# A row LSTM on one Trainium2 core: image preparation dealt out anew at the start, one more odd output kept in PSUM, one wait placed earlier

## The chip, the cores and the metric

The kernel runs on one core of one Trainium2 chip. The metric is device time in microseconds (us); less is better. Before the change it is 1946.57 us, the median of 3 runs (1944.31 to 1946.65). All times below are in us unless marked ns.

## The reference

```
x : (8, 96, 128, 128) float32
v   = group_norm(x, 32 groups, no affine)
its = conv_1x3(v, W_is * mask) + b_is          # along the row, causal mask, 4*96 channels
for each of the 128 image rows:                # lax.scan, carry h, c : (8, 96, 128)
    gates = conv_1x3(h, W_ss) + b_ss + its[row]
    f, i, o = sigmoid(three quarters); g = tanh(the fourth)
    c = f * c + i * g
    h = o * tanh(c)
out = x + h of every row
```

The recurrence over the 128 rows is the long part: each row needs the hidden state of the row above.

## The kernel before

**Tiling and halves.** The eight images are split into two halves of four (s = 0 and 1). A half-step is one row of one half; half-step n is row n/2 of a half, with the first half one row ahead (`LEAD = 1`, `place`, lines 443 to 448). There are 256 half-steps, numbered from -2, and the two halves alternate, so that one half's products run on TensorE beside the other half's gates. Channels lie on the partitions: 96 partitions of hidden state `hx`, and 32 partitions that hold normalised input channels ("shared" channels) so that one product contracts both. Even and odd pixels are separate; the 1x3 convolution is computed from sums and differences of them with fewer products: `vs` (total, S), `vf` (difference, F), `vo` (shifted odd differences, D1) and `ve` (shifted even differences, D0, in `te`). The rest of the input channels arrive as "own" images `xs`: for each image of a block of four rows, a widening normalisation (`widen`, line 349), a sum (`add_pixels`, line 366) and a difference (`subtract_pixels`, line 370), all on GpSimd.

**Half-step.** Three PSUM banks A, B, C collect the gates. Products named 0, 1, 2, 3 take `vo`, `vs`, `vf`, `ve`; P, Q, E take the own images. Each is cut in two by row groups of 64 partitions ("lanes", marked < and >), so two products run side by side. ScalarE copies a bank's left half with the bias (`copy`, cp, line 620); VectorE then makes the even half (`even`, lo, line 624) and the odd half (`odd`, hi, line 628), and the 0 and 3 products are added to them after that. Then come the sigmoids and tanhs on ScalarE (lines 633, 654, 659), the cell on VectorE (`forget` 664, `gated` 673, `cell` 686), with the even pixels' input product on GpSimd from half-step 3 on (`gated`, line 671), tanh of the cell (694), and the outputs (703). From half-step 2 on ("banked") the odd output is left in PSUM: ScalarE copies it from there into `hx` (`keep_odd`, co, line 714), and copies the shared odd channels beside it (`shared_odd`, uo, line 719), so that S and F of the next row read one operand from PSUM.

**Order.** The instruction order of TensorE, ScalarE, VectorE and GpSimd is written by hand; each engine takes its instructions in that order. SyncE's DMA queue is ordered by the framework. A string `PERIOD` lists what one pass does; pass (period) n mixes the products of half-steps n and n+1 (marked +) with the gates of n-1 (marked '). It begins `siBb' 2C< taCb' U loA taCa' hiA cpB siC' PA+> gtb' QB+< 2C> 0A<`. Here `U` is the place where the shared images listed for half-step n-1 are normalised, W3 the place of the last piece of n-1's own image and of the loads listed behind it ("rest"), W1+ and W2+ the first two pieces of n's own image. S', F', D1' and D0' make the operands of half-step n+1. Passes 2 to 253 run this string; the last half-steps run another one, and half-steps -2 to 1 are written out by hand between the statistics of the last images (`events`) and in a few `do(...)` lines after them.

**Image work.** `work(n)` says which shared images, which own image and which loads belong to half-step n. For n under 8 it comes from the table `FIRST`, otherwise from a rule; `LATER` adds three more pieces, for the first own image of the second half's next block, in passes 10, 12 and 14. `shared(...)` gives an image to GpSimd (line 349, written to `hx`), `beside(...)` to ScalarE (line 347). `finish(0)` and `finish(1)` do the own images of half-steps 0 and 1 in one go.

**Waits.** An instruction carries one wait on another engine; what else it has to wait for is put in a separate instruction ahead of it on its queue. In each of the passes 3 to 253 the product `0A<` waits for VectorE (hiA) in such a separate instruction and for GpSimd (`vo`) itself, and `2C<` has no wait of its own. `follow(a, b)` adds a wait of a for b.

## Time and profile before

| | |
|---|---|
| median of 3 runs | 1946.57 us (1944.31 to 1946.65) |
| profiled execution | 1946.32 us |
| its span, first to last instruction | 1944.5 us |
| mean granted TensorE clock | 0.993 |
| TensorE busy (PE, matmul records) | 1868.6 us, 96%, 16400 records |
| VectorE (DVE) busy | 1558.2 us, 80% |
| ScalarE (ACT) busy | 1677.9 us, 86% |
| GpSimd (POOL) busy | 1567.9 us, 81% |
| DMA | 242.87 MB, 125 GB/s in the mean |

How to read it: PE is TensorE's matmuls, PEld its weight loads (a float32 product leaves two records of each), SP is SyncE, which issues DMAs. In a timeline a row gives start, duration, engine, line of the kernel (L628), operation, output<-inputs, their shapes, and how many like it are merged (x2); in square brackets stand the idle time of the engine just before it and what ended that. In the chain of waits a row gives start, duration and what ran. In the table by stretch a row gives the stretch, its length, then for PE, PEld, DVE, ACT and POOL the busy time with the number of instructions, then the granted clock (1.00 is full speed), the DMA share and GB/s. In the list of DMA issues the last figure is the median time from issue to landing. The statistics of the eight images take about the first 140 us; the half-steps of the main order follow.

### The profile page before, as it was taken

The page shows a single profiled execution, that of the slowest core. Times are in us where ns is not written, and L with a number is a line of the kernel's source. Part 1 is how long each engine was busy: PE and PEld are TensorE (multiplying, and loading weights), DVE is VectorE, ACT ScalarE, POOL GpSimd, SP SyncE. Part 2 cuts the span into 40 slices and gives each one's busy share as a digit, 9 for nine tenths or more (in the row PEclk, how much of TensorE's full clock was granted, in tenths as well). Part 3 has the DMA queues.
Part 4 walks back from the last instruction along what each step waited for, and adds up shares of the span by engine and source line. Part 5 has one row for each costly group of instructions (what it writes and reads, how often), then busy time and mean ns, then how long its engine had stood idle before and what let it go on. Part 6 is the DMA issues. An engine that isn't in the chain of part 4 may idle for free.

```text
span 1944.5 us, 46633 instructions
## 1 busy us (share of the span) xinstructions
PE 1868.6 (96%) x16400; PEld 1736.9 (89%) x16400; DVE 1558.2 (80%) x4018; ACT 1677.9 (86%) x3961; POOL 1567.9 (81%) x2169
## 2 busy tenths in 40 slices
PE   3778999999999999999999999999999999999998
PEld 0447999999999999999999999999999999999996
DVE  5877888888888888888888888888888888888886
ACT  6687888888888888888888888888888888888887
POOL 4347888888888888888888888888888888888862
PEclk9989999999999999999999999999999999999999
DMA  9994344334434443444344334434443444344301
GB/s 405 413 303 101 90 120 123 104 96 124 114 93 105 124 113 99 109 121 106 88 120 123 104 97 122 115 92 105 123 113 98 109 121 109 86 121 123 93 28 45
DMA packets 110294, 242.87 MB, mean 125 GB/s; under 512 B 6832, under 2 KB 16368, under 8 KB 104048
## 3 DMA queue, kind: packets, MB, share of 16 engines
q1 hardware_dynamic: 110064, 239.89, 44.2%
q8 instruction: 133, 2.18, 0.5%
q14 instruction: 97, 0.79, 0.1%
HBM read 181.34 MB, written 50.33 MB: 119 GB/s over the span
## 4 chain that ended last, share of the span: by engine, by line
PE 92%; DMA 3%; DVE 2%; ACT 2%; POOL 1%; issue 0%; SPq 0%; DVEq 0%; POOLq 0%; ACTq 0%
PE ps L548 92%; DMA x<-in_x_dram 2%; DVE bst L1215 1%; DMA te<-in_x_dram 1%; POOL xw L349 0%; ACT g L633 0%; POOL xs L366 0%; PE rows L224 0%; ACT ps L654 0%; POOL xs L370 0%; PE pv L303 0%; POOL hx L349 0%; ACT o L659 0%; ACT xr L235 0%; ACT hx L268 0%
## 5 line engine op out<-in xcount | busy, mean ns | idle before, releaser
L548 PE MATMUL ps<-te,wl 64*128 64x256 f32 (+1 forms) x3042 | 911.6, 380 | 0.2
L548 PE MATMUL ps<-vf,wm 64*128 64x256 f32 (+1 forms) x3046 | 782.1, 382 | 0.1
L548 PE MATMUL ps<-vo,wl 64*128 64x256 f32 (+1 forms) x3042 | 738.3, 385 | 6.0 <-DVE ps L628 5.9
L548 PE MATMUL ps<-xs,wx 64*128 64x256 f32 (+1 forms) x3080 | 699.8, 377 | 2.1 <-POOL xs L366 1.8
L548 PE MATMUL ps<-vs,wm 64*128 64x256 f32 (+1 forms) x3046 | 658.0, 378 | 9.8 <-POOL vs L739 7.1
L548 PEld LDWEIGHTS ps<-te,wl 64*128 64x128 f32 (+1 forms) x3042 | 520.3, 186 | 42.5 <-PE ps L548 1.4
L624 DVE TENSOR_TENSOR ps<-m,ps 128x256 f32<-128x256 f32 x768 | 323.5, 421 | 279.4 <-ACT m L620 279.3
L548 PEld LDWEIGHTS ps<-xs,wx 64*128 64x128 f32 x3080 | 492.2, 187 | 14.5 <-POOL xs L366 3.4
L548 PEld LDWEIGHTS ps<-vo,wl 64*128 64x128 f32 (+1 forms) x3042 | 487.3, 186 | 18.0 <-DVE ps L628 8.4
L548 PEld LDWEIGHTS ps<-vf,wm 64*128 64x128 f32 (+1 forms) x3046 | 442.8, 185 | 32.1 <-PE ps L548 0.9
L548 PEld LDWEIGHTS ps<-vs,wm 64*128 64x128 f32 (+1 forms) x3046 | 446.5, 188 | 16.1 <-POOL vs L739 9.9
L620 ACT ACTIVATE m<-ps,wl 128x256 f32<-128x256 f32 x766 | 360.0, 470 | 24.9 <-PE ps L548 11.9
L633 ACT ACTIVATE g<-ps 32x512 f32<-32x512 f32 x765 | 317.9, 447 | 45.0 <-PE ps L548 10.2
L628 DVE TENSOR_TENSOR ps<-m,ps 128x256 f32<-128x256 f32 x768 | 325.5, 424 | 17.6
L548 PE MATMUL ps<-xs,wt 64*128 64x256 f32 x1012 | 299.2, 376 | 1.4 <-DVE ps L628 1.4
L370 POOL TENSOR_TENSOR xs<-xw 128x512 f32<-128x512 f32 (+1 forms) x254 | 294.0, 1158 | 0.1
L671 POOL TENSOR_TENSOR g<-i,g 96x256 f32<-96x256 f32 x251 | 182.4, 727 | 138.2 <-ACT g L633 137.9
L654 ACT ACTIVATE ps<-ps 96x512 f32<-96x512 f32 (+1 forms) x512 | 243.3, 475 | 45.5 <-PE ps L548 45.1
L349 POOL TENSOR_SCALAR xw<-xr,rstd,nmr 128x512 f32<-128x512 f32 (+1 forms) x267 | 210.3, 789 | 36.5 <-DVE nmr L341 11.5
L694 ACT ACTIVATE ps<-c 96x256 f32<-96x256 f32 x512 | 193.2, 378 | 40.1 <-DVE c L686 3.7
L753 POOL TENSOR_TENSOR vo<-hx 128x256 f32<-128x256 f32 x257 | 157.3, 612 | 84.4 <-ACT hx L714 74.9
L349 POOL TENSOR_SCALAR hx<-x,rstd,nmr 32x512 f32<-32x512 f32 x245 | 199.1, 813 | 27.5 <-ACT hx L347 2.1
(132 smaller groups left out, 2661.3 us busy)
## 6 DMA issues: line engine op xcount, KB each, us to landing
xr<-in_x_dram SPq DMA_DIRECT2D x124, 512.0 KB, 6.3
x<-in_x_dram SPq DMA_DIRECT2D x62, 768.0 KB, 4.9
out_dram<-x SPq DMA_DIRECT2D x62, 768.0 KB, 4.6
x<-in_x_dram SPq DMA_DIRECT2D x16, 1024.0 KB, 10.8
x<-in_x_dram SPq DMA_DIRECT2D x62, 256.0 KB, 2.9
xs<-in_x_dram SPq DMA_DIRECT2D x15, 1024.0 KB, 12.2
te<-in_x_dram SPq DMA_DIRECT2D x8, 1024.0 KB, 11.1
hx<-in_x_dram SPq DMA_DIRECT2D x8, 1024.0 KB, 9.6
```

Of the source, the lines that this page charges most:

```text
L349: return engine.tensor_scalar(dst, src, scale, shift, ALU.mult, ALU.add)
L370: return engine.tensor_sub(differences, strided(xw[:, 0, :], 0, [(W + 1, n), (J + 1, 2), (1, J)]), strided(xw[:, 0, :], J, [(W + 1, n), (0 ...
L548: made = nc.tensor.matmul(self.ps[a][:, bass.ts(half, HB)][:, cols], weights[rows, bass.ts(a, P)], rhs[rows, cols], start=new, stop=False, ...
L620: nc.scalar.activation(self.m1[a], m1, AF.Identity, bias=column)
L624: nc.vector.tensor_add(self.ps[a][:, 0:HB], self.m1[a], self.ps[a][:, HB:])
L628: nc.vector.tensor_sub(hi, self.m1[a], hi)
L633: made = nc.scalar.activation(self.part(g, lo, hi, t), self.part(ps, lo, hi, t), AF.Tanh)
L654: made = nc.scalar.activation(to, gate, AF.Sigmoid)
L671: nc.gpsimd.tensor_mul(to, i, g)
L694: nc.scalar.activation(th, self.part(self.c, lo, hi, t), AF.Tanh)
L753: nc.gpsimd.tensor_sub(to, h[:, :, 0:J], h[:, :, 1 : J + 1])
L1215: nc.vector.bn_stats(bst[:, done, :], xc[:, bass.ts(j, SN)])
```

## The change

Three edits.

1. The table `FIRST` and what follows it: no image is given to ScalarE any more (`beside` is gone); the own and shared images of half-steps 0 to 7 are dealt out differently; the first own image of the second half's next block (image 3 of block 1) is cut into three pieces that follow in passes 4, 5 and 6, image 1 of the first half's block 2 into pieces in passes 9, 10, 11, and image 0 of the second half's block 2 in passes 12, 13, 14. Two loads (`spare`, `load_rows` of the second half) move to the list of half-step 6, those of the first half from half-step 1 to 3.
2. `banked` from half-step 1 instead of 2, with `co uo` written into the hand order of half-step 1 after `ou`, ahead of F and S.
3. The first 2C product of each half-step waits for `vo`, the odd differences of GpSimd that `0A<` of the same half-step needs later.

```diff
-            self.banked = self.n >= NH
+            self.banked = self.n >= 1
...
+            if kind == "2" and a == order["C"] and first is None and "vo" in self.kept:
+                follow(self.made, self.kept["vo"], "the odd differences are there")
...
-            nc.gpsimd.tensor_sub(to, h[:, :, 0:J], h[:, :, 1 : J + 1])
+            self.kept["vo"] = nc.gpsimd.tensor_sub(to, h[:, :, 0:J], h[:, :, 1 : J + 1])
...
-    def beside(s, k, *images):
-        return shared(s, k, *images, engine=nc.scalar)
-
     FIRST = [
-        ([], own(0, 1, 1), own(0, 1, 2)),
-        (shared(0, 1, 0), own(0, 1, 3), [(spare, 0, 1), (load_rows, 0, 2)]),
-        (beside(0, 1, 1) + shared(0, 1, 2) + beside(0, 1, 3), own(1, 1, 0), [(load_shared, 0, 2)]),
-        (shared(1, 1, 0), own(1, 1, 1), []),
-        (beside(1, 1, 1) + shared(1, 1, 2), own(1, 1, 2), []),
-        (shared(1, 1, 3), own(1, 1, 3), [(spare, 1, 1), (load_rows, 1, 2), (load_shared, 1, 2)]),
-        (shared(0, 2, *SHARED[0]), own(0, 2, 0), [(load_shared, 0, 3)]),
-        ([], own(0, 2, 1), []),
+        ([], own(0, 1, 1), []),
+        (shared(0, 1, 0, 1), (), []),
+        (shared(0, 1, 2), own(0, 1, 2), [(load_shared, 0, 2)]),
+        (shared(0, 1, 3), own(0, 1, 3), [(spare, 0, 1), (load_rows, 0, 2)]),
+        (shared(1, 1, 0), own(1, 1, 0), []),
+        (shared(1, 1, 1), own(1, 1, 1), [(load_shared, 1, 2)]),
+        (shared(1, 1, 2) + shared(0, 2, 0), own(1, 1, 2), [(load_shared, 0, 3)]),
+        (shared(1, 1, 3), own(0, 2, 0), []),
     ]
-    LATER = dict(zip((9, 11, 13), own(1, 2, 0, 1)))
+    LATER = dict(
+        [*zip((3, 4, 5), own(1, 1, 3, 1)), *zip((8, 9, 10), own(0, 2, 1, 1)),
+         *zip((11, 12, 13), own(1, 2, 0, 1))]
+    )
+    BLOCK = {6: [(spare, 1, 1), (load_rows, 1, 2)]}
...
-            return FIRST[n]
+            channels, image, rest = FIRST[n]
+            return channels, image, rest + ([LATER[n]] if n in LATER else []) + BLOCK.get(n, [])
...
-    do(1, "gt th 0+A 3+A 0+B 3+B 0+C 3+C ou F S D0 D1 re")
+    do(1, "gt th 0+A 3+A 0+B 3+B 0+C 3+C ou co uo F S D0 D1 re")
```

`own(s, k, j, buffer)` returns the three pieces of own image j of block k of half s, `shared(s, k, j, ...)` the normalisations of shared images, as listed in the kernel above.

## The prediction

> **What bounds the kernel now.** I read the page first, then the engines' busy times by stretch, then the chain of waits from 155 to 200 us, then the timelines of the single engines there and in a later stretch for comparison.

> ```profile
> span 1944.5 us, 46633 instructions
> 160.00:170.00 10.00, 6.79 (x46) 5.82 (x47) 5.96 (x16) 6.94 (x15) 6.44 (x9) 0.90 0.87 181
> 168.00:169.00 1.00, 1.00 (x7) 0.95 (x6) 0.97 (x4) 0.97 (x3) 0.10 (x1) 0.50 1.10 211
> 180.00:190.00 10.00, 9.16 (x80) 8.16 (x80) 7.33 (x20) 8.52 (x20) 7.51 (x10) 1.00 0.27 64
> 400.00:800.00 400.00, 400.00 (x3655) 380.82 (x3653) 325.59 (x857) 352.18 (x857) 344.73 (x457) 1.00 0.41 107
> ```

> In the steady stretch (400 to 800) TensorE is never idle. From 160 to 190, in periods 3 to 6 of the hand-written order, it is: 46 matmul records between 160 and 170 where the steady stretch has 91 in ten microseconds, and between 168 and 169 the granted clock is 0.50. So an edit to the steady order has little to win, and the edits to periods 2 to 16 are priced in that start.

> The clearest ruler is line 628 for bank B (hiB), which runs once a period and lets the next odd products go:

> ```profile
> 166.41 0.42 DVE L628 TENSOR_TENSOR ps<-m,ps 128x256 f32<-128x256 f32 x1
> 174.95 0.41 DVE L628 TENSOR_TENSOR ps<-m,ps 128x256 f32<-128x256 f32 x1
> 183.49 0.41 DVE L628 TENSOR_TENSOR ps<-m,ps 128x256 f32<-128x256 f32 x1
> 190.50 0.42 DVE L628 TENSOR_TENSOR ps<-m,ps 128x256 f32<-128x256 f32 x1
> 246.55 0.42 DVE L628 TENSOR_TENSOR ps<-m,ps 128x256 f32<-128x256 f32 x1
> 253.81 0.42 DVE L628 TENSOR_TENSOR ps<-m,ps 128x256 f32<-128x256 f32 x1
> 260.81 0.41 DVE L628 TENSOR_TENSOR ps<-m,ps 128x256 f32<-128x256 f32 x1
> ```

> These are periods 3, 4, 5, 6, 14, 15 and 16. From 6 to 14 eight periods take 56.05, so a good period is 7.01. Period 4 takes 8.54 (1.53 too long), period 5 again 8.54 (1.53 too long), period 15 takes 7.26 (0.25 too long). The chain of waits says why periods 3 and 5 are late:

> ```profile
> 162.96 0.82 POOL hx L349
> 163.80 0.84 ACT hx L347
> 164.66 0.39 ACT g L633
> ...
> 180.49 0.85 ACT hx L347
> ...
> 181.50 0.81 POOL hx L349
> ...
> 182.40 0.73 POOL g L671
> ```

> ScalarE's share of the shared-channel images (L347, the helper "beside") writes the same tile as GpSimd's (L349), and each waits for the other in turn. The tanh (L633) that the cell needs stands behind them on ScalarE's queue.

> **The change part by part.**

> *The "beside" images go to GpSimd.* In period 3 the queues of ScalarE, VectorE and TensorE read:

> ```profile
> 160.54 0.38 ACT L633 ACTIVATE g<-ps 64x256 f32<-64x256 f32 x1
> 161.09 0.41 DVE L673 TENSOR_TENSOR g<-ps,g 96x256 f32<-96x256 f32 x1
> 166.88 0.70 PE L548 MATMUL ps<-vo,wl 64*128 64x256 f32 x4 [3.21 <-DVE ps L628]
> ```

> Without the two images the second tanh starts when the first ends, at 160.54 + 0.38 = 160.92 instead of 164.66: 3.74 earlier. VectorE then does gtb (161.09, done about 161.5) and goes on without its pause; the same chain of five VectorE operations leads to hiB, about 0.1 less is won because gtb stands in front, and another 0.1 goes to the PSUM edit below. That puts hiB at 162.9 instead of 166.41: 3.5 won. It cannot be less than about 3.2 (the idle time that TensorE's row shows) unless another wait takes the place, nor more than 3.7. What is late next is nothing: bank B's copy, which hiB also needs, follows the tanh on ScalarE as before. In period 5 the same pair (ScalarE 180.49, GpSimd 181.50, and the product 182.40 behind it) costs the 1.53 of that period; it goes too, because ScalarE has no image any more and GpSimd waits for none.

> *The clock.* Period 4 has no wait of its own; its 1.53 is the stretch at clock 0.50 that follows TensorE's 3.21 idle. Period 5's shorter stall leaves the clock at 1.00 (the row 180 to 190). So without the 3.21 I take the 1.53 as won; its ends are 0 and 1.53. [...]

> *GpSimd's new load.* It gets ScalarE's three images (0.81 to 0.85 each, on either engine) and the first images of the second half, one piece more in periods 4 (widen), 5 (add) and 6 (subtract), then 9, 10, 11 and 12, 13, 14; period 7 has two shared images in front of its gate product. What a piece too many does is shown by period 14, which has one subtraction more already:

> ```profile
> 245.41 0.73 POOL L671 TENSOR_TENSOR g<-i,g 96x256 f32<-96x256 f32 x1 [0.48 <-ACT g L633]
> ...
> 246.80 2.28 POOL L370 TENSOR_TENSOR xs<-xw 128x512 f32<-128x512 f32 x2
> 249.06 0.82 POOL L349 TENSOR_SCALAR xw<-xr,rstd,nmr 128x512 f32<-128x512 f32 x1
> ...
> 250.97 0.75 POOL L366 TENSOR_TENSOR xs<-xw 128x256 f32<-128x256 f32 x1
> 251.82 0.81 POOL L349 TENSOR_SCALAR hx<-x,rstd,nmr 32x512 f32<-32x512 f32 x1
> 252.71 0.72 POOL L671 TENSOR_TENSOR g<-i,g 96x256 f32<-96x256 f32 x1
> 253.47 0.42 DVE L686 TENSOR_TENSOR c<-ps,g 96x256 f32<-96x256 f32 x1 [0.15 <-POOL g L671]
> ```

> From gate product to gate product GpSimd needs 7.30 here without a pause, so 7.30 - 1.14 = 6.16 without the second subtraction (2.28 / 2), and 0.85 is free in a good period. The product came 0.29 late (7.30 - 7.01), VectorE waited for it, and hiB lost 0.25. So lateness of the gate product costs nearly its own length.
> - Periods 4 and 5: one widen (0.82) or one add (0.75) on 6.16 is at most 6.98, under 7.01: nothing.
> - Period 6 into 7: a subtraction (1.14) and a second shared image (0.81, with its handover 0.85) give 6.16 + 1.99 = 8.15. The product is 1.14 late, about 1.1 lost. Bounds: 0.7 if the pauses ahead can be worked into, 2 if every added piece costs 0.2 more.
> - Period 11 into 12: again 7.30, 0.25 lost, new. Period 14 into 15 is as before.

> *The odd output of half-step 1 stays in PSUM.* VectorE's last operations before TensorE goes on with the products of half-step 3, and the later forms:

> ```profile
> 155.08 0.75 DVE L703 TENSOR_TENSOR hx<-o,ps 96x256 f32<-96x256 f32 x2 [0.78 <-ACT ps L694]
> 155.86 1.18 DVE L743 TENSOR_TENSOR vf<-hx 128x256 f32<-128x256 f32 x1
> 156.96 0.41 DVE L739 TENSOR_TENSOR vs<-hx 128x256 f32<-128x256 f32 x1
> 166.99 0.38 ACT L719 ACTIVATE ps<-hx 32x256 f32<-32x256 f32 x1
> 176.46 0.42 DVE L743 TENSOR_TENSOR vf<-ps,hx 128x256 f32<-128x256 f32 x1
> ```

> Added are two ScalarE copies of 0.38 between the output products (they end at 155.83) and the difference; the difference falls from 1.18 to 0.42 with one operand in PSUM. 155.83 + 2 x 0.38 + 0.33 (the step from one such VectorE operation to the next) + 0.42 + some 0.2 of handovers is 157.54 against the 157.37 at which the sum ends now: 0.1 to 0.2 lost, already in the 3.5. I take 0.42, the row with the same operands; were the PSUM form as slow as 1.18 here, 0.9 would be lost. [...] The copies push the ScalarE work of half-step 2 back by about 1.3; ScalarE stands idle 2.45 after it, so nobody waits:

> ```profile
> 159.79 0.47 ACT L620 ACTIVATE m<-ps,wl 128x256 f32<-128x256 f32 x1 [2.45 <-PE ps L548]
> ```

> *The wait on GpSimd's odd differences moves from the odd product 0A to the first 2C product,* in every period. The separate VectorE wait in front of 0A goes, since one wait then fits the matmul itself.

> ```profile
> 312.45 0.61 POOL L753 TENSOR_TENSOR vo<-hx 128x256 f32<-128x256 f32 x1 [0.26 <-ACT hx L714]
> 314.75 0.34 PEld L548 LDWEIGHTS ps<-vf,wm 64*128 64x128 f32 x4
> 315.63 0.18 PEld L548 LDWEIGHTS ps<-vo,wl 64*128 64x128 f32 x1
> 603.10 0.38 PE L548 MATMUL ps<-vo,wl 64*128 64x256 f32 x1
> 606.77 0.38 PE L548 MATMUL ps<-vf,wm 64*128 64x256 f32 x1
> ```

> The differences end at 313.06 and the loads of 2C are at 314.75: 1.7 to spare (2.6 before), and even a GpSimd 1.1 late keeps 0.6. Queued behind the waiting product are all of TensorE's further products. From 603.10 (the first record of a 0A) to 606.77 TensorE starts 34 records, 0.1079 each; over the whole steady stretch it is 400 / 3655 = 0.1094. So all of TensorE's waits together take 64 x 0.0015 = 0.1 of a period of 64 records: the ends are -0.1 and +0.1 a period. I take 0, because both waits at 0A are met before its load is due.

> *Transfers.* The first block's spare rows and next rows go out later, in periods 4 and 7 on SyncE's queue:

> ```profile
> xr<-in_x_dram SPq DMA_DIRECT2D x124, 512.0 KB, 6.3
> ```

> They land in about 6.3 and are first read two periods (14) or more afterwards. Hidden; if they took over 13, GpSimd would wait.

> **Sum.** 3.5 + 1.53 + 1.53 - 1.1 - 0.25 = 5.2 won, against the profiled execution's 1946.32 (span 1944.5 and 1.8 around it): 1941.1. That run is 0.25 under the median of 1946.57, so 1941.4 for a median. A measurement here can tell about 0.2% (3.9) from no change.

> **The rivals.**
> - *GpSimd becomes the bound of the start.* Nine periods carry an added piece; if each costs 0.2 more than its row, periods 4, 5, 9 to 14 overrun too, by 0.1 to 0.25 each, and period 7 by 2. The win falls to 2.5 to 3.8: 1942.8 to 1944. For it: the free 0.85 lies in two pauses that ScalarE's results set. Against: periods 10 and 12 carry a piece more already, and from 6 to 14 the eight periods are all of 7.01 in the mean. Chance 0.18.
> - *The clock falls anyway:* the stretch at 0.50 belongs not to the 3.21 but to all of TensorE's idle time since 140, which stays in part. 1.5 less, 1942.9. For it: no row quoted here shows a second stall of that length with the same consequence. Against: the row 168 to 169 stands right behind the stall's end at 166.88. Chance 0.07. [...]
> - *The stall of period 7 hides* (GpSimd works ahead), or the shorter wait list speeds the steady order a little: 1939 to 1940. Chance 0.08.
> - *Slower: the moved wait is paid every period.* 2C's load comes where the queue has just waited for the other lane, so what stands there is not hidden. A wait of w adds 251 w, over periods 3 to 253. It decides from (5.2 + 3.9)/251 = 0.036; at 0.1, as much as all waits of a period now cost, it is 25 - 5.2, 1966. Against: the differences are 1.7 early, and a wait that is met shows no gap at 0A. Chance 0.05.
> - *The change does not do it:* the period 3 stall stays because GpSimd's own images stand before the gate product there. But that product is VectorE's in period 3. Chance 0.02.

> **How the numbers follow.** Forecast (1939.8 to 1942.7) 0.60. Faster: 0.60 + 0.08 and a small part of the first two rivals, 0.70. Same: the rest of these and the unchanged case, 0.25. Slower 0.05. The range takes the forecast, the third case and most of the first two: 1939.0 to 1944.6.

> **What would show it.** In the profile after: hiB of period 3 near 163 and no idle row of over 1 us before an odd product until period 7; no granted clock under 1.00 after 145; no ScalarE images of 32x512 after 152; a VectorE wait of about 1 us on GpSimd's gate product near 191; the difference at 0.42 near 156.8. The steady period stays 7.01. It is wrong if the period changes, if the clock still falls near 168, or if the periods 4 to 6 show waits on GpSimd.

## The result, and the profile after

| | before | after |
|---|---|---|
| median, nine runs each on one chip | 1945.49 us (1944.31 to 1946.84) | 1940.21 us (1939.25 to 1941.34) |
| profiled execution (its span) | 1946.32 (1944.5) | 1941.34 (1939.5) |
| mean granted clock | 0.993 | 0.994 |
| instructions | 46633 | 46380 |

The ratio is 0.9973, 95% interval 0.9964 to 0.9982: the changed kernel is faster by 0.27%, 5.3 us. In the kernel after, lines 620 to 771 stand two further down, so the bank B ruler (hiB, line 628) is L630 and the gate product of GpSimd (line 671) is L673.

The table by stretch of the kernel after, columns as before:

```profile
160.00:170.00 10.00, 9.94 (x82) 8.75 (x82) 7.37 (x20) 7.88 (x20) 7.67 (x10) 1.00 0.32 78
168.00:169.00 1.00, 1.00 (x12) 0.96 (x10) 0.06 (x1) 0.99 (x4) 0.90 (x3) 1.00 1.12 246
...
180.00:190.00 10.00, 10.00 (x95) 9.48 (x93) 7.72 (x21) 8.82 (x21) 9.69 (x14) 1.00 0.26 79
190.00:200.00 10.00, 9.67 (x85) 8.64 (x84) 7.56 (x20) 8.01 (x21) 8.90 (x12) 1.00 0.93 204
400.00:800.00 400.00, 400.00 (x3658) 380.87 (x3657) 325.18 (x857) 352.27 (x857) 344.81 (x458) 1.00 0.42 108
```

The hole between 160 and 170 is mostly closed (82 matmul records in place of 46), the half-rate microsecond at 168 is at 1.00, and 180 to 190 has the 95 records of a good stretch. (A row of ten microseconds counts records that begin before it too, so a full one has 95 and not the 91 of the long stretch, which the prediction set beside the 46.) One hole is left, or rather new: 190 to 200 has 85 records, ten too few, so about 1.1 us lost (10 x 0.11). The idle column there shows only 0.33 us. While one lane waits the last products of the other still run: one lane's end at 193.22 and the other's, on `te`, at 193.60, and the next record begins at 193.94, 0.72 behind the last start, where the steady stretch has 0.11. So the count of records is the better measure of this short stall.

The ruler, VectorE's timeline of the kernel after:

```profile
145.42 1.09 DVE L630 TENSOR_TENSOR ps<-m,ps 128x256 f32<-128x256 f32 x3
...
164.42 0.42 DVE L630 TENSOR_TENSOR ps<-m,ps 128x256 f32<-128x256 f32 x1
...
171.42 0.42 DVE L630 TENSOR_TENSOR ps<-m,ps 128x256 f32<-128x256 f32 x1
...
178.42 0.41 DVE L630 TENSOR_TENSOR ps<-m,ps 128x256 f32<-128x256 f32 x1
...
185.42 0.41 DVE L630 TENSOR_TENSOR ps<-m,ps 128x256 f32<-128x256 f32 x1
...
193.47 0.41 DVE L630 TENSOR_TENSOR ps<-m,ps 128x256 f32<-128x256 f32 x1
...
221.48 0.42 DVE L630 TENSOR_TENSOR ps<-m,ps 128x256 f32<-128x256 f32 x1
...
228.74 0.41 DVE L630 TENSOR_TENSOR ps<-m,ps 128x256 f32<-128x256 f32 x1
...
242.74 0.42 DVE L630 TENSOR_TENSOR ps<-m,ps 128x256 f32<-128x256 f32 x1
...
250.00 0.42 DVE L630 TENSOR_TENSOR ps<-m,ps 128x256 f32<-128x256 f32 x1
```

The hiB of period 2 is the second of the three in the first row, at 145.75; then follow those of periods 3, 4, 5, 6, 7, 11, 12, 14 and 15. Periods 4, 5 and 6 take 7.00 each; 7 takes 8.05, 12 takes 7.26 (228.74 - 221.48), 15 takes 7.26. In the kernel before, the hiB of period 2 is the second of the three in this row of VectorE, at 144.16:

```profile
143.83 1.08 DVE L628 TENSOR_TENSOR ps<-m,ps 128x256 f32<-128x256 f32 x3
```

So the main order begins 1.6 later in the profiled execution of after, for a reason that is not the change (last section). Absolute times of the two traces may not be set against each other; lengths from hiB to hiB may. That is the measure of everything below. From hiB of period 2 to that of period 17 before takes 123.66 and after 118.25: 5.41 won.

### The profile page after: what moved, and what is told of

The parts are those of the page before. It is cut to its first block, busy times and chain, and to the rows that moved or that the text cites. A ratio compares the mean times of both kernels' runs of the same rounds, so it can differ in the third digit from the quotient of the medians.

```text
span 1939.5 us, 46380 instructions
## 1 busy us (share of the span) xinstructions
PE 1866.1 (96%) x16400; PEld 1736.1 (90%) x16400; DVE 1554.4 (80%) x4018; ACT 1676.1 (86%) x3960; POOL 1567.1 (81%) x2172
## 4 chain that ended last, share of the span: by engine, by line
PE 92%; DMA 3%; ACT 2%; DVE 1%; POOL 1%; issue 0%; SPq 0%; DVEq 0%; POOLq 0%; ACTq 0%
PE ps L548 92%; DMA x<-in_x_dram 2%; DVE bst L1219 1%; DMA te<-in_x_dram 1%; POOL xw L349 0%; ACT g L635 0%; POOL xs L370 0%; ACT ps L656 0%; ACT x L269 0%; ACT x L268 0%; POOL xs L366 0%; PE pv L303 0%; ACT m L622 0%; ACT ps L696 0%; ACT o L661 0%
## 5 line engine op out<-in xcount | busy, mean ns | idle before, releaser
L548 PE MATMUL ps<-te,wl 64*128 64x256 f32 (+1 forms) x3042 | 909.6, 379 | 0.2
L548 PE MATMUL ps<-vf,wm 64*128 64x256 f32 (+1 forms) x3046 | 783.6, 382 | 0.1
L548 PE MATMUL ps<-vo,wl 64*128 64x256 f32 (+1 forms) x3042 | 736.4, 384 | 2.3 <-DVE ps L630 2.2
L548 PE MATMUL ps<-xs,wx 64*128 64x256 f32 (+1 forms) x3080 | 700.0, 377 | 3.4 <-POOL xs L366 1.8
L548 PE MATMUL ps<-vs,wm 64*128 64x256 f32 (+1 forms) x3046 | 657.8, 378 | 10.7 <-POOL vs L741 7.9
L548 PEld LDWEIGHTS ps<-te,wl 64*128 64x128 f32 (+1 forms) x3042 | 519.7, 185 | 42.6 <-PE ps L548 1.4
L548 PEld LDWEIGHTS ps<-vo,wl 64*128 64x128 f32 (+1 forms) x3042 | 495.7, 186 | 13.7 <-DVE ps L630 4.4
L548 PEld LDWEIGHTS ps<-xs,wx 64*128 64x128 f32 x3080 | 492.2, 187 | 16.2 <-POOL xs L366 3.4
L548 PEld LDWEIGHTS ps<-vf,wm 64*128 64x128 f32 (+1 forms) x3046 | 443.5, 186 | 32.2 <-PE ps L548 0.9
L548 PEld LDWEIGHTS ps<-vs,wm 64*128 64x128 f32 (+1 forms) x3046 | 445.9, 188 | 17.0 <-POOL vs L741 10.4
L630 DVE TENSOR_TENSOR ps<-m,ps 128x256 f32<-128x256 f32 x768 | 325.5, 424 | 17.6
L548 PE MATMUL ps<-xs,wt 64*128 64x256 f32 x1012 | 299.2, 376 | 1.4 <-DVE ps L630 1.4
L370 POOL TENSOR_TENSOR xs<-xw 128x512 f32<-128x512 f32 (+1 forms) x254 | 293.0, 1154 | 0.1
L673 POOL TENSOR_TENSOR g<-i,g 96x256 f32<-96x256 f32 x251 | 182.0, 725 | 133.7 <-ACT g L635 133.1
L349 POOL TENSOR_SCALAR xw<-xr,rstd,nmr 128x512 f32<-128x512 f32 (+1 forms) x267 | 209.3, 785 | 35.7 <-DVE nmr L341 11.5
L349 POOL TENSOR_SCALAR hx<-x,rstd,nmr 32x512 f32<-32x512 f32 x248 | 201.3, 812 | 25.8
## 6 DMA issues: line engine op xcount, KB each, us to landing
xr<-in_x_dram SPq DMA_DIRECT2D x124, 512.0 KB, 6.4
```

The costliest lines, as they stand in the source:

```text
L349: return engine.tensor_scalar(dst, src, scale, shift, ALU.mult, ALU.add)
L370: return engine.tensor_sub(differences, strided(xw[:, 0, :], 0, [(W + 1, n), (J + 1, 2), (1, J)]), strided(xw[:, 0, :], J, [(W + 1, n), (0 ...
L548: made = nc.tensor.matmul(self.ps[a][:, bass.ts(half, HB)][:, cols], weights[rows, bass.ts(a, P)], rhs[rows, cols], start=new, stop=False, ...
L630: nc.vector.tensor_sub(hi, self.m1[a], hi)
L673: nc.gpsimd.tensor_mul(to, i, g)
```

## The experiments

Theory A: the stall of period 3 and the clock that falls behind it, and the stall of period 5, all come from the two engines that write the shared images in turn (edit 1); GpSimd's extra pieces give 1.3 of it back; edits 2 and 3 are nearly nothing. Rivals: the gain is owed to the moved wait or to the odd output; the clock falls for another reason than the stall; the new order of the images, and not the engine that writes them, does it. After is set against the nine runs of before in the first table, wait only to after without wait against 25 other runs of it (median 1946.92), filled stall to engine only against 26 more (1945.63).

| kernel | median us (runs) | ratio to before, 95% | period 3 | 4 | 5 | 7 | 8 | 12 | 15 | 3 to 17 |
|---|---|---|---|---|---|---|---|---|---|---|
| before | | | 22.25 | 8.53 | 8.55 | 7.01 | 7.01 | 7.01 | 7.25 | 123.66 |
| after | 1940.21 (9) | 0.9973 (0.9964 to 0.9982) | 18.66 | 7.00 | 7.00 | 8.04 | 7.00 | 7.26 | 7.26 | 118.25 |
| wait only | 1946.11 (11) | 0.9998 (0.9989 to 1.0006) | 22.25 | 8.56 | 8.55 | 7.00 | 7.00 | 7.01 | 7.26 | 123.66 |
| table only | 1940.35 (5) | 0.9968 (0.9955 to 0.9980) | 18.59 | 7.00 | 7.00 | 8.05 | 7.00 | 7.26 | 7.27 | 118.21 |
| odd output only | 1945.75 (11) | 0.9995 (0.9986 to 1.0004) | 21.99 | 8.55 | 8.55 | 7.01 | 7.00 | 7.00 | 7.26 | 123.40 |
| after without wait | 1941.70 (9) | 0.9976 (0.9966 to 0.9985) | 18.66 | 7.00 | 7.00 | 8.06 | 7.00 | 7.27 | 7.26 | 118.28 |
| filled stall | 1944.38 (11) | 0.9994 (0.9985 to 1.0003) | 22.26 | 7.00 | 8.56 | 7.01 | 7.00 | 7.01 | 7.25 | 122.13 |
| one image later | 1941.12 (10) | 0.9975 (0.9966 to 0.9984) | 18.66 | 7.00 | 7.01 | 7.26 | 7.26 | 7.26 | 7.26 | 117.74 |
| spread | 1939.02 (5) | 0.9966 (0.9953 to 0.9978) | 18.66 | 7.01 | 7.00 | 7.00 | 7.01 | 7.00 | 7.01 | 116.74 |
| engine only | 1941.71 (11) | 0.9979 (0.9971 to 0.9988) | 18.59 | 8.93 | 7.35 | 7.01 | 7.00 | 7.00 | 7.26 | 119.18 |

The lengths are from one trace of each kernel, worked out from the unrounded starts of hiB. They repeat within 0.03 in kernels that have the same order there, while the medians of the three sets of runs of before alone lie 1.4 apart; so small effects are read from the lengths, and the medians only confirm the large ones.

**Wait only**: the kernel before with edit 3 alone.

```diff
+            if kind == "2" and a == order["C"] and first is None and "vo" in self.kept:
+                follow(self.made, self.kept["vo"], "the odd differences are there")
...
+            self.kept["vo"] = nc.gpsimd.tensor_sub(to, h[:, :, 0:J], h[:, :, 1 : J + 1])
```

> The kernel before with the third edit alone: the first 2C product of each half-step waits for the odd differences. Theory A (the wait is free at both places): the period from one line-628 subtraction of bank B to the next stays at 7.01 us as before, periods 3, 4, 5 keep their stalls, and the time is within 0.3 us of before. Theory B (the separate wait that goes shortens the steady order; the profile after shows many periods of 7.00 where before had 7.004 and 7.009): periods of 7.00, about 0.005 x 250 = 1.2 us less than before. Theory C (the new wait is paid each time): periods of 7.04 or more, 9 us or more above before.

This kernel has 46382 instructions, 251 fewer than before, so the separate waits of the 251 passes did go. The ratio's interval allows at most 0.0011 x 1946 / 251 = 0.009 won and 0.0006 x 1946 / 251 = 0.005 lost in each of the 251 periods. The rival "paid every period" needed 0.036 and is out. So is the idea that this edit carries the gain.

**Table only**: the kernel after without edits 2 and 3.

```diff
-            self.banked = self.n >= 1
+            self.banked = self.n >= NH
...
-            if kind == "2" and a == order["C"] and first is None and "vo" in self.kept:
-                follow(self.made, self.kept["vo"], "the odd differences are there")
...
-    do(1, "gt th 0+A 3+A 0+B 3+B 0+C 3+C ou co uo F S D0 D1 re")
+    do(1, "gt th 0+A 3+A 0+B 3+B 0+C 3+C ou F S D0 D1 re")
```

> The kernel before with the first edit alone (no images on ScalarE, the new table). Theory A (the table makes all of the gain): line 628 of bank B takes 18.6 us from period 2 to 3 (22.25 before), 7.01 in periods 4, 5 and 6, about 8.05 in period 7 and 7.26 in periods 12 and 15; the granted clock stays at 1.00 after the statistics; the time is 5 to 5.5 us under before, a little more than with all three edits if keeping the odd output costs 0.1. Rival (the odd output kept in PSUM makes a part of it): at most 4 us under before.

From hiB 2 to hiB 17 it takes 118.21, and after 118.25. Edit 1 is the whole gain. Period 3 is 0.07 shorter than in after: that is the price of edit 2 where the stall is gone.

**Odd output only**: the kernel before with edit 2 alone.

```diff
-            self.banked = self.n >= NH
+            self.banked = self.n >= 1
...
-    do(1, "gt th 0+A 3+A 0+B 3+B 0+C 3+C ou F S D0 D1 re")
+    do(1, "gt th 0+A 3+A 0+B 3+B 0+C 3+C ou co uo F S D0 D1 re")
```

> The kernel before with the second edit alone (half-step 1 leaves its odd output in PSUM). Theory A: the difference of half-step 3 takes 0.42 us in place of 1.18, two ScalarE copies of 0.38 stand ahead of it, TensorE goes on with the sums 0.1 us later; the stalls of periods 3 and 5 and the half-rate stretch stay; time within 0.3 us of before. Rival (the shorter difference lets half-step 3 begin earlier): TensorE goes on 0.5 us or more earlier and the time falls by that.

Period 3 became 0.26 shorter. Two more copies stand on the way to the difference, and yet it is shorter, since in this order GpSimd's chain sets the end of the period. The timelines of VectorE and of GpSimd in this kernel, then GpSimd's in the kernel before:

```profile
156.75 0.42 DVE L743 TENSOR_TENSOR vf<-ps,hx 128x256 f32<-128x256 f32 x1 [0.86 <-ACT ps L719]
```

```profile
156.98 0.80 POOL L349 TENSOR_SCALAR xw<-xr,rstd,nmr 128x512 f32<-128x512 f32 x1
```

```profile
155.58 0.61 POOL L749 TENSOR_TENSOR te<-hx 96x256 f32<-96x256 f32 x1 [0.43 <-DVE hx L703]
156.15 0.61 POOL L753 TENSOR_TENSOR vo<-hx 128x256 f32<-128x256 f32 x1
156.75 1.22 POOL L349 TENSOR_SCALAR xw<-xr,rstd,nmr 128x512 f32<-128x512 f32 x1
```

The same widening on GpSimd takes 1.22 beside VectorE's difference of two SBUF operands (155.86 for 1.18) and 0.80 beside the one with an operand in PSUM (0.42). In this one meeting both took longer. It ends 0.19 earlier by these rows (156.75 + 1.22 against 156.98 + 0.80), in a trace whose period 2 ended 0.07 later; the sum is the 0.26. In the kernel after, GpSimd is not the last in period 3, so the gain is not there and the 0.07 is.

**After without wait**: the kernel after without edit 3.

```diff
-            if kind == "2" and a == order["C"] and first is None and "vo" in self.kept:
-                follow(self.made, self.kept["vo"], "the odd differences are there")
```

> The kernel after without the third edit. Theory A (the third edit does nothing): periods as in the profile after, 7.000 and 7.004 mixed, and the time within 0.3 us of the kernel after. Theory B (the third edit shortens the period): periods of 7.004 and 7.009 as before, and about 1.2 us more than the kernel after, that is 4 us under before.

118.28 against 118.25. The ratio interval overlaps after's for nearly its whole length. Whether edit 3 is worth some tenths of a microsecond stays open: the mean period from 17 to 247 is 7.0043, 7.0063, 7.0080 and 7.0070 in the four traces with it, and 7.0095, 7.0070, 7.0077, 7.0069, 7.0072 and 7.0083 in the six without it. The means of the two groups differ by 0.0014, 0.3 us in 230 periods, less than the spread within either.

**Filled stall**: the kernel before, with seven products of zeros put on TensorE into the stall of period 3, so that it waits as long but is not idle. They add zeros to a bank.

```diff
+    zeros = const.tile([P, BH * J], F32, name="zeros")
+    nc.gpsimd.memset(zeros, 0.0)
...
+        if n == 3:
+            ahead, behind = PERIOD.split("0B< ")
+            do(n, ahead, by_lanes=True)
+            for i in range(FILL):
+                half_step(n + 1).mm(order["A"], 0, wt[0], zeros)
+            do(n, "0B< " + behind, by_lanes=True)
+            continue
```

> The kernel before with seven products of zeros (whole height, added to a bank of half-step 4, 0.43 us each) put on TensorE ahead of the product that stalls in period 3, so that TensorE works through the stall of 3.2 us; the stall's cause stays. Theory A (the idle stretch makes the clock fall): period 3 stays at 22.2 to 22.3 us, no half-rate stretch follows near 168, period 4 falls from 8.54 to 7.0 to 7.1 us, period 5 keeps its 8.54; 1.5 us less from period 2 to the end. Rival (the clock falls by itself or by the idle time since 140): the stretch of 3.41 us at half rate stays and period 4 takes 8.5 us.

TensorE's timeline (line 548 is L552 in this kernel), then the table by stretch:

```profile
163.37 3.29 PE L552 MATMUL ps<-zeros,wl 128*128 128x256 f32 x14
166.65 0.70 PE L552 MATMUL ps<-vo,wl 64*128 64x256 f32 x4
```

```profile
166.00:170.00 4.00, 4.00 (x33) 3.29 (x32) 3.69 (x10) 3.31 (x8) 1.33 (x3) 1.00 1.07 203
```

Period 3 is as long as before (22.26), the clock stays at 1.00 and period 4 takes 7.00: exactly the 1.53 went, and nothing else. So it was the idle time of this stall that made the clock fall, not the stall as such. The rival that the rate falls anyway is out: the rest of TensorE's idle time since 140 was still there.

**One image later**: the kernel after, with the second shared image of period 7 moved into period 8, so that no period holds two added pieces.

```diff
-        (shared(1, 1, 2) + shared(0, 2, 0), own(1, 1, 2), [(load_shared, 0, 3)]),
-        (shared(1, 1, 3), own(0, 2, 0), []),
+        (shared(1, 1, 2), own(1, 1, 2), [(load_shared, 0, 3)]),
+        (shared(1, 1, 3) + shared(0, 2, 0), own(0, 2, 0), []),
```

> The kernel after with one shared image (0 of the first half's block 2) moved from period 7 to period 8. Theory A (lateness of GpSimd's gate product costs its own length, 0.85 us a period are free): period 7 takes 7.25 us (8.04 in the kernel after), period 8 takes 7.00 to 7.02 although it has two images now, 0.8 us less in all. Rival (two images in one period cost 0.8 us wherever they stand): period 8 takes 7.8 us and nothing is won.

Period 7 fell to 7.26, as a second subtraction by itself costs. But period 8 is 7.26 too, so only 0.50 was won in all. That is the place where the "0.85 free" of the prediction should have held an image of 0.81. GpSimd's timeline in this kernel, periods 8 and 9:

```profile
197.25 1.62 POOL L349 TENSOR_SCALAR hx<-x,rstd,nmr 32x512 f32<-32x512 f32 x2
198.95 0.72 POOL L673 TENSOR_TENSOR g<-i,g 96x256 f32<-96x256 f32 x1
...
205.92 0.72 POOL L673 TENSOR_TENSOR g<-i,g 96x256 f32<-96x256 f32 x1 [0.58 <-ACT g L635]
```

and in the steady part of the kernel after, the two places where GpSimd stands in a good period:

```profile
602.77 0.61 POOL L755 TENSOR_TENSOR vo<-hx 128x256 f32<-128x256 f32 x1 [0.28 <-ACT hx L716]
...
606.04 0.73 POOL L673 TENSOR_TENSOR g<-i,g 96x256 f32<-96x256 f32 x1 [0.47 <-ACT g L635]
```

The free time is two pauses: 0.28 ahead of `vo`, which waits for ScalarE's copy of the odd output, and 0.47 to 0.58 ahead of the gate product. A piece that stands before `vo` can use both. A shared image stands behind `vo` and can use only the second: 0.81 - 0.58 = 0.23 is late by the row of period 9, 0.81 - 0.47 = 0.34 by the steady one; 0.26 was measured. This account fits the rows, but no run moved an image from behind `vo` to ahead of it.

**Spread**: the kernel after, with the shared images one half-step earlier, so that none of the periods 4 to 7 has two, and the extra own images (image 3 of the second half's block 1, then images 1 and 0 of the two halves' block 2) cut into four pieces (the subtraction in two halves), over passes 3 to 6, 8 to 11 and 12 to 15.

```diff
-        (shared(0, 1, 2), own(0, 1, 2), [(load_shared, 0, 2)]),
-        (shared(0, 1, 3), own(0, 1, 3), [(spare, 0, 1), (load_rows, 0, 2)]),
-        (shared(1, 1, 0), own(1, 1, 0), []),
-        (shared(1, 1, 1), own(1, 1, 1), [(load_shared, 1, 2)]),
-        (shared(1, 1, 2) + shared(0, 2, 0), own(1, 1, 2), [(load_shared, 0, 3)]),
-        (shared(1, 1, 3), own(0, 2, 0), []),
+        (shared(0, 1, 2, 3), own(0, 1, 2), [(load_shared, 0, 2)]),
+        (shared(1, 1, 0), own(0, 1, 3), [(spare, 0, 1), (load_rows, 0, 2)]),
+        (shared(1, 1, 1), own(1, 1, 0), []),
+        (shared(1, 1, 2), own(1, 1, 1), [(load_shared, 1, 2)]),
+        (shared(1, 1, 3), own(1, 1, 2), [(load_shared, 0, 3)]),
+        (shared(0, 2, 0), own(0, 2, 0), []),
...
+    def in_four(s, k, j):
+        first, second, (_, wide, _, differences) = own(s, k, j, 1)
+        return first, second, (subtract_one, wide, differences, 1), (subtract_one, wide, differences, 0)
...
-        [*zip((3, 4, 5), own(1, 1, 3, 1)), *zip((8, 9, 10), own(0, 2, 1, 1)),
-         *zip((11, 12, 13), own(1, 2, 0, 1))]
+        [*zip((2, 3, 4, 5), in_four(1, 1, 3)), *zip((7, 8, 9, 10), in_four(0, 2, 1)),
+         *zip((11, 12, 13, 14), in_four(1, 2, 0))]
```

> The kernel after with the shared images of periods 3 to 8 one period earlier (two in period 3, where VectorE makes the gate product, then one each) and the three extra own images cut into four pieces, the subtraction of 1.16 us as two of 0.73. Theory A: no period has more than 6.16 + 0.82 us of GpSimd work, so periods 3 to 16 all take 7.00 to 7.02 us but period 3 itself (18.6); 1.5 us less than the kernel after from period 2 to the end. Rival (another wait stands right behind GpSimd's): periods 7, 12 and 15 stay above 7.1.

Every period from 4 to 17 takes 7.00 or 7.01; from hiB 2 to hiB 17 it is 116.74, 1.51 less than after. The table by stretch, where after had 85 records, and GpSimd's timeline at an added half subtraction (L814):

```profile
190.00:200.00 10.00, 10.00 (x96) 9.57 (x93) 8.56 (x24) 8.77 (x23) 9.06 (x12) 1.00 0.81 172
```

```profile
183.61 1.16 POOL L370 TENSOR_TENSOR xs<-xw 128x512 f32<-128x512 f32 x1
184.73 0.75 POOL L814 TENSOR_TENSOR xs<-xw 128x256 f32<-128x256 f32 x1
...
189.23 0.72 POOL L673 TENSOR_TENSOR g<-i,g 96x256 f32<-96x256 f32 x1 [0.20 <-ACT g L635]
```

A half of 0.75 fits where a whole of 1.14 does not, and the gate product still waits 0.20 for ScalarE instead of being late. By its lengths this is the best version. Its median is the lowest of all, but it was timed in another set of runs than after, and the two intervals overlap.

**Engine only**: the kernel before, whose table stays as it is; the images of ScalarE go to GpSimd.

```diff
-        return shared(s, k, *images, engine=nc.scalar)
+        return shared(s, k, *images)
```

> The kernel before with ScalarE's three shared images given to GpSimd at the same places, all else of the old table kept. Theory A (ScalarE's queue made the stalls, and GpSimd's load then sets the new ones): period 3 takes 18.6 us, the clock stays at 1.00, period 4 takes about 8.9 us because GpSimd is about 2 us late with the gate product (three images and an own image ahead of it), period 5 takes 7.0 to 7.1; 4.5 to 5 us less than before from period 2 to the end, so that the new order of the table is worth 1 to 1.5 us. Rival (the new order of the table is what wins): less than 2 us under before.

From hiB 2 to hiB 17 this wins 123.66 - 119.18 = 4.48 of the 5.41. So the engine is most of it, and the new order of the table the remaining 0.9. Period 4 came as expected (8.93); period 5 takes 7.35 where 7.0 to 7.1 was expected. GpSimd's timeline around period 5 shows the same as one image later: two images behind `vo`, the product at 179.70 without a pause, and 0.61 of a pause again one period on.

```profile
177.91 1.71 POOL L349 TENSOR_SCALAR hx<-x,rstd,nmr 32x512 f32<-32x512 f32 x2
179.70 0.73 POOL L671 TENSOR_TENSOR g<-i,g 96x256 f32<-96x256 f32 x1
...
186.67 0.73 POOL L671 TENSOR_TENSOR g<-i,g 96x256 f32<-96x256 f32 x1 [0.61 <-ACT g L633]
```

## Why the prediction was right, step by step

The forecast was 1941.4, 5.2 won; measured were 5.41 in periods 3 to 17, 5.3 by the medians, and 1940.21. Most of the 1.2 between 1941.4 and 1940.21 is the start of the sum: nine runs of before have their median at 1945.49, 1.1 under that of the three runs shown.

| term | predicted | measured | by |
|---|---|---|---|
| period 3, the wait of the two engines for each other | +3.5 (3.2 to 3.7) | +3.59 | 22.25 - 18.66 |
| clock in period 4 | +1.53 | +1.53 | 8.53 - 7.00 |
| period 5, the same pair | +1.53 | +1.55 | 8.55 - 7.00 |
| period 7, two added pieces | -1.1 (0.7 to 2) | -1.03 | 7.01 - 8.04 |
| period 12, second subtraction | -0.25 | -0.25 | 7.01 - 7.26 |
| odd output in PSUM (inside the 3.5) | -0.1 to -0.2 | -0.07 | 18.59 - 18.66, table only against after |
| moved wait | 0 | not told from 0 | wait only |

The remaining 0.02 of the 5.41 is thousandths in the other ten periods, less than the traces can tell.

**Period 3.** ScalarE's timeline of the kernel before shows what the 3.74 of the prediction are made of, and GpSimd's shows the other direction, in period 5:

```profile
161.17 0.85 ACT L347 ACTIVATE hx<-x,nmr,rstd 32x512 f32<-32x512 f32 x1 [0.25 <-POOL hx L349]
163.80 0.84 ACT L347 ACTIVATE hx<-x,nmr,rstd 32x512 f32<-32x512 f32 x1 [1.79 <-POOL hx L349]
```

```profile
181.50 0.81 POOL L349 TENSOR_SCALAR hx<-x,rstd,nmr 32x512 f32<-32x512 f32 x1 [2.09 <-ACT hx L347]
```

In period 3 ScalarE waits 0.25 and 1.79 for GpSimd, 2.04 in all, and the two images themselves take 1.69 of its queue ahead of the tanh. So the wait for each other, under which the table has the whole term, is somewhat over half of it; the rest is the images' own time. Giving them to GpSimd takes both away, and no run here lifts the order between the two engines and leaves the images on ScalarE. In period 5 it is GpSimd that waits, 2.09.

In the kernel after, ScalarE writes no shared image beside GpSimd: its last images, by the view of line 347, belong to half-step 1, which is written out by hand, and none of them is 32x512.

```profile
L347 ACT ACTIVATE hx<-x,nmr,rstd x4: 721/731/742, 148.9 to 151.2; 32x384 f32<-32x384 f32 x4
```

"What is late next is nothing" held: VectorE goes through the chain that the prediction followed, and period 3 takes 18.66. Engine only, which has edit 1's engine and nothing else of it, has the same 18.59 as table only; that is 3.66 under before, and the odd output takes 0.07 of it back.

**The clock.** The step was right, and filling the stall shows it: with TensorE at work through the stall the clock stays at 1.00 (the row 166 to 170 there). In the kernel before, the rate fell to 0.50 after 3.21 of idle time and stayed down for 3.41 (167.94 to 171.35); in the kernel after, it stayed at 1.00 behind an idle time of 1.44 (ahead of half-step 3's products, below).

**Period 7.** The prediction's chain can be read off line by line. GpSimd's timeline of the kernel after, then VectorE's, then TensorE's:

```profile
184.29 0.73 POOL L673 TENSOR_TENSOR g<-i,g 96x256 f32<-96x256 f32 x1 [0.21 <-ACT g L635]
...
185.67 2.27 POOL L370 TENSOR_TENSOR xs<-xw 128x512 f32<-128x512 f32 x2
...
190.69 1.60 POOL L349 TENSOR_SCALAR hx<-x,rstd,nmr 32x512 f32<-32x512 f32 x2
192.37 0.72 POOL L673 TENSOR_TENSOR g<-i,g 96x256 f32<-96x256 f32 x1
```

```profile
193.12 0.42 DVE L688 TENSOR_TENSOR c<-ps,g 96x256 f32<-96x256 f32 x1 [0.94 <-POOL g L673]
```

```profile
193.94 0.70 PE L548 MATMUL ps<-vo,wl 64*128 64x256 f32 x4 [0.33 <-DVE ps L630]
```

From product to product GpSimd takes 8.08 (192.37 - 184.29) without a pause, where 8.15 was forecast; VectorE waits 0.94, hiB loses 1.03. The sum was right because this period has a piece on each side of `vo`, and so uses both pauses. The step "0.85 is free" itself was wrong as a general statement: one image later and engine only, which were costed with it, each had a period a quarter to a third of a microsecond longer than expected. The forecast took no harm from it because the added pieces of periods 4 and 5 stand ahead of `vo`; the sum did not ask where they stand, so there it was lucky.

**The odd output.** The row with the same operands was the right one to take. VectorE's difference and TensorE's next products in the kernel after:

```profile
158.29 0.42 DVE L745 TENSOR_TENSOR vf<-ps,hx 128x256 f32<-128x256 f32 x1 [0.86 <-ACT ps L721]
158.63 0.41 DVE L741 TENSOR_TENSOR vs<-hx,ps 128x256 f32<-128x256 f32 x1
```

```profile
159.09 0.70 PE L548 MATMUL ps<-vs,wm 64*128 64x256 f32 x4 [1.44 <-DVE vs L741]
```

What the prediction missed is the other side of the same meeting: it counted the 1.18 of VectorE, and not the 1.22 of GpSimd's widening beside it. In the order before that is worth 0.26, in the order after nothing. The rows before have it on both engines: the difference, of two operands in SBUF, begins at 155.86 inside GpSimd's `te` (155.58 to 156.19), has `vo` of GpSimd (156.15 for 0.61) inside it too, and takes 1.18, where the form with an operand in PSUM takes 0.42; the widening begins at 156.75 inside the difference (155.86 to 157.04) and takes 1.22, beside that other form 0.80. No run here separated the operations, so what makes both long was not shown.

**The rivals.** GpSimd as the bound of the whole start: periods 4, 5, 9, 10, 11, 13 and 14 carry an added piece and take 7.00, so it falls. The clock that falls anyway: out by the filled stall. A hidden stall in period 7: it costs 1.03. A faster steady order: 7.0043 against 7.0095 in the profiled pair, but kernels with the same steady order differ by as much as 0.0037 (7.0043 and 7.0080, both with edit 3), so at most a part of it can be owed to the edit. The moved wait paid every period: out. The change that doesn't do what it says: out.

## What to carry to other kernels

Two engines that write parts of one tile can be ordered one behind the other, and then a helper that was given work to relieve a busy engine stalls both, with everything queued behind them (here ScalarE waited 2.04 in period 3 and GpSimd 2.09 in period 5); giving all writes of the tile to one engine won 4.5 of 5.4 us here, even with more work on that engine. A stall is priced by the record count of its stretch (1.1 here where the idle column has 0.33) and by what the clock does behind it (1.53 behind the 3.21), not by the idle column alone. "Free" time on an engine was a list of pauses here (0.28, and 0.47 to 0.58), each at a place in its queue: by this account a piece fits only if the pauses behind it, up to the next point that others wait for, are as long as the piece, so cut pieces to the pauses (0.75 fitted where 1.14 didn't).

## What the runs showed of the hardware besides

**The start differs from run to run by more than the edits 2 and 3 are worth.** hiB of period 2 lies between 142.94 (table only) and 145.93 (engine only) in the ten traces, and not by kernel: wait only, which has the statistics phase of before, is at 145.65. The granted clock between 120 and 145 goes with it in nine of them: 0.86 where hiB comes at 142.94 to 144.23, 0.80 where it comes at 145.65 to 145.93; spread has 0.80 at 143.69. The table by stretch of table only and then of after:

```profile
120.00:145.00 25.00, 20.71 (x103) 14.15 (x100) 21.56 (x58) 21.67 (x36) 13.24 (x32) 0.86 0.90 247
```

```profile
120.00:145.00 25.00, 18.89 (x83) 13.87 (x80) 21.15 (x54) 19.99 (x33) 10.48 (x28) 0.80 0.94 273
```

Which is cause and which effect is open; no run here set the two apart.

**A few steady periods are longer by a fixed amount**: 7.06 in place of 7.00 at half-steps 31, 94, 157 and 220 of after, 63 apart, and 7.21 at 76 and 213. Before has such periods 8 half-steps later (39, 102, 165, 228; 7.06 to 7.07), and 7.23 at 83 and 7.22 at 220. The cause is open.
